# Projecting queries and keys of one batch at a time, in blocks of 256 columns

## The chip, the core and the metric

The kernel runs on one core of a Trainium2 chip, in one launch. The metric is the device time in microseconds (us) of that core, the median of repeated executions. Engines are named as in the profile: PE (TensorE, the matrix engine; PEld is its loading of stationary operands), DVE (VectorE), ACT (ScalarE), POOL (GpSimd) and SP (SyncE, which here only issues transfers). All data of this kernel are float32 unless said otherwise, and the engines wait for one another through semaphores.

## The reference, cut to what matters

The computation is a decoder of two layers on x of shape (8, 256, 512): eight batches of 256 tokens, 512 features. Each step is added to x and the sum is normalised over the features:

```python
x = _layernorm(x + _L0_attn_ref(x, ...))    # differential attention, causal
x = _layernorm(x + _L0_xattn_ref(x, ...))   # long convolution, with the context
x = _layernorm(x + _L0_ffn_ref(x, ...))     # experts, two for each token
x = _layernorm(x + _L1_attn_ref(x, ...))    # causal self attention, 16 heads of 32
x = _layernorm(x + _L1_xattn_ref(x, ...))   # cross attention
x = _layernorm(x + _L1_ffn_ref(x, ...))     # routed causal attention
```

The two stages that the change touches are both causal attentions. The first has 32 query heads of 16 features (taken in pairs, of which the second is subtracted with a learned factor) and 8 heads of keys; the self attention has 16 heads of 32:

```python
qkv = jnp.einsum('bsd,ed->bse', x, w_qkv)
q, k, v = ...                                   # 16 heads of 32 each
scores = jnp.einsum('bhqd,bhkd->bhqk', q, k) * HD ** (-0.5)
scores = jnp.where(causal, jnp.float32(-1000000000.0), scores)
a = jax.nn.softmax(scores, axis=-1)
ctx = jnp.einsum('bhqk,bhkd->bhqd', a, v)
return jnp.einsum('bsd,ed->bse', ctx.reshape(b, s, d), w_o)
```

## The kernel before, in words

**Tiles.** The 2048 tokens are 16 tiles x0 to x15 of 128 tokens by 512 features (P = 128, D = 512, KB = 4 blocks of 128 features, NT = 16). A batch is two tiles (S = 256 tokens), a group is two batches, so four tiles (TPG = 4, GT = 512 tokens), and there are four groups (NG = 4).

**Stages.** In the trace the first attention takes the span from 0 to about 490 us, the long convolution to 830, the experts to 1115, the self attention from 1115 to 1502, the cross attention to 1843, the routed attention the rest.

**Units and slots.** `causal_attention` (L1097) serves the three causal attentions. A unit is four heads of one batch: eight units to a batch in the first attention (`upb` 8), four in the self attention. The program runs through slots; in slot u it lays out for PE: the scores of unit u for the maxima (`maxima`, ps_q, L1151), the transposed weights of the unit `wait` slots before (`weights`, ps_k, L1214 and L1223), and the products with the values of the unit one slot before that (`products`, ps_pv, L1257 and L1267). Around a unit the other engines work: ACT copies the scores from PSUM to `rows` (L1160), POOL masks `rows` (affine_select, L1162), DVE takes the negated maximum `neg` (L1171); later ACT takes the exponential `pT` (L1231), POOL masks it (L1232), DVE takes the reciprocal sum (L1275). After the last unit of a batch `split` (L1178 to L1185) cuts the maxima into bfloat16 terms, and `turn` (ps_n, L1193) turns them on PE for the weights of that batch. The PSUM tile of the scores has one buffer, shared by ps_q and ps_k; `rows` has two buffers in the first attention and one in the self attention.

**Filling.** The projections of a group are a list of pieces, each with a slot by which it must have run and a list of steps (one matmul each, with an assumed cost). `prepare` makes the list. Pieces wait in `queue`, ordered by that due slot; `fill` puts steps into PE's order between scores, weights and products as long as a budget lasts; `need` runs what is due in the next slot. `at` registers other work for a place of a later slot ("start", "mid", "end"), or as output projections for "fill". So the order of the instructions on PE, DVE, ACT and POOL is written out by the program, and each of these engines executes in that order. SP's transfers are ordered by the scheduler.

**Projections.** Each group is turned: four transposes on PE to a tile, one PSUM tile `pt`, one ACT copy to `xT` (L195; `turned_group`, with one buffer for xT). `feature_block` (L1404) computes 128 output features for all 512 tokens of the group: four matmuls of 128x512, evicted by ACT (L1411) to qT or kT. In the first attention keys are one such block `ps_k`, evicted twice by ACT to `kz` with a mask `half` of one or the other half of each pair of heads (L323). Values are computed by tile.

**The start of the program.** `load_x` (L67) has SP load tiles 0 to 3; then Wk, Wq, Wv and Wo follow (L131, L248). Wq is reordered by eight copies on DVE (L269) and eight on POOL (L271) before queries can use it; `half` (L275) is reduced on DVE.

**The start of the self attention.** The experts leave their outputs in DRAM (`ys`). `combine` (L1064) makes three functions for a tile: `load` (SP loads x from DRAM, L1075, and POOL gathers two rows of ys for each token, L1077), `add` (two DVE additions L1086, then DVE statistics and two POOL instructions for the root, L139 and L140), and `norm` (DVE, L154). `self_attention` (L1437) does this for tiles 0 to 3 before the first slot. In `prepare` of group g the tiles of group g + 1 are registered one after the other: for the first group tiles 4 and 5 are gathered at the end of slot 0, tile 6 at the end of slot 1, tile 7 at the end of slot 2. The query and key blocks of column block c are due in slot c, the values of the first batch in slot 5, of the second in slot 7 (9 in the last group).

Of the kernel before, what the change touches and what calls it, by code (L numbers as in the profile page):

```python
# [5 lines left out]


# [2 lines left out]

# [6 lines left out]
F32 = mybir.dt.float32  # L17
# [6 lines left out]
P = 128  # L24
B, S, D = 8, 256, 512
NT = B * S // P
TPG = 4
NG = NT // TPG
GT = TPG * P
KB = D // P  # L30
# [3 lines left out]
H0, HD0 = 16, 16  # L34
LAMBDA_INIT = 0.8 - 0.6 * math.exp(-0.3 * 12)
H1, HD1 = 16, 32
# [13 lines left out]
def decoder_kernel(ctx: ExitStack, tc: tile.TileContext, a: dict, out: bass.AP):  # L50
    nc = tc.nc
# [15 lines left out]
    def load_x(tiles):  # L67
        for t in tiles:
            nc.sync.dma_start(out=x[t], in_=xin[:, t, :])

    load_x(range(TPG))

    ident = const.tile([P, P], F32, tag="ident", name="ident")
    make_identity(nc, ident)
# [97 lines left out]

    MM, TR = 0.86, 0.45

    def product_steps(tile, lhsT, rhs, done):

        ps = []

        def step(k):
            if k == 0:  # L180
                ps.append(tile())
            nc.tensor.matmul(  # L182
                ps[0], lhsT=lhsT(k), rhs=rhs(k), start=(k == 0), stop=(k == KB - 1)
            )
            if k == KB - 1:
                done(ps[0])

        return [(MM, lambda k=k: step(k)) for k in range(KB)]

    def turned(pools, dst, src, tag="mm"):  # L190

# [43 lines left out]
    def diff_attention():  # L235
# [6 lines left out]
        w = wpool.tile([P, 7168], F32, tag="w", name="w_l0")  # L242
        wk = load_w(w, 2048, a["L0_attn_Wk"], P)
        wq_in = load_w(w, 0, a["L0_attn_Wq"], D)
        wv = load_w(w, 2560, a["L0_attn_Wv"], P)
        wo = w[:, 3072:5120].rearrange("p (k c) -> p k c", k=KB)
        for t in range(4):
# [15 lines left out]
        wq = w[:, 5120:7168].rearrange("p (k c) -> p k c", k=KB)  # L263
# [35 lines left out]
        def prepare(work, pools, g, at, here):  # L299
            qT = work.tile([P, KB, GT], F32, tag="qT", name="qT")  # L300
            kz = work.tile([P, 2, GT], F32, tag="kz", name="kz")
            v = work.tile([P, TPG, P], F32, tag="v", name="v", bufs=3)
            xT, need = turned_group(work, pools, g)
# [12 lines left out]
            values_steps = [(MM, lambda ti=ti: values(ti)) for ti in range(TPG)]  # L316
            if g:

                need.append((0, values_steps))

            def keys(ps):
                for i in range(2):
                    nc.scalar.mul(kz[:, i, :], ps, half[:, i : i + 1])  # L323

            need.append(
                (
                    0,
                    product_steps(
                        lambda: pools.tile([P, GT], F32, tag="mm", name="ps_k"),
                        lambda k: wk[:, k, :],  # L330
                        lambda k: xT[0][:, k, :],
                        keys,
                    ),
                )
            )
            for c, first in enumerate((0, 1, 4, 5)):
                need.append((first, feature_block(pools, qT, xT, wq, 0, c, HD0**-0.5)))

            if g == 0:
                need.append((9, values_steps))  # L340
# [756 lines left out]
    def causal_attention(name, prepare, finish, upb=KB, gather=None):  # L1097
# [18 lines left out]
        with ExitStack() as st:  # L1116
# [175 lines left out]
            due = [0]  # L1292

            def at(slots, place, f):

                if place == "fill":
# [104 lines left out]
                fill(9.0)  # L1401
                happen("end")

    def feature_block(pools, r, xT, w, at, c, scale=1.0):  # L1404

        cs = slice(at + c * P, at + (c + 1) * P)
        return product_steps(
            lambda: pools.tile([P, GT], F32, tag="mm", name="ps_f"),
            lambda k: w[:, k, cs],
            lambda k: xT[0][:, k, :],  # L1410
            lambda ps: nc.scalar.mul(r[:, c, :], ps, scale),  # L1411
        )
# [23 lines left out]

    def self_attention(wqkv, wo, arrive):  # L1437

        for steps in zip(*[arrive(t) for t in range(TPG)]):
            for f in steps:  # L1440
                f()

        def prepare(work, pools, g, at, here):
            qT = work.tile([P, KB, GT], F32, tag="qT", name="qT")
            kT = work.tile([P, KB, GT], F32, tag="kT", name="kT")
            v = work.tile([P, TPG, D], F32, tag="v", name="v_s")
            xT, need = turned_group(work, pools, g)
            for c in range(KB):
                need.append((c, feature_block(pools, qT, xT, wqkv, 0, c, HD1**-0.5)))
                need.append((c, feature_block(pools, kT, xT, wqkv, D, c)))  # L1450

            if g + 1 < NG:
                for ti in range(TPG):
                    load, add, norm = arrive((g + 1) * TPG + ti)
                    first = max(0, 2 * KB * g - 1 + ti)
                    at(first - here, "end", load)
                    at(first - here + 1, "mid", lambda add=add: add(lambda f: at(0, "end", f)))
                    at(first - here + 2, "mid", norm)

            for ti in range(TPG):  # L1460
                need.append(
                    (
                        5 + ti // 2 * (4 if g == NG - 1 else 2),
                        token_block(
                            pools, xT, wqkv, 2 * D, ti,
                            lambda ps, ti=ti: nc.scalar.copy(v[:, ti, :], ps),
                        ),
                    )
                )
# [12 lines left out]

        causal_attention("s", prepare, finish)


# [257 lines left out]
    with ExitStack() as st_self:  # L1743
# [111 lines left out]
```

## Time and profile before

| What | us |
|---|---|
| Time before, median of 3 runs | 2199.62 (2196.56 to 2202.16) |
| The profiled execution, its own time | 2202.62 |
| Its span in the trace | 2200.8 |
| PE busy in it | 2053.4 (93%) |
| DVE, POOL, ACT busy | 1272.1, 824.4, 598.9 |
| Mean granted clock of PE | 0.97 |
| First attention, 0 to 490: PE busy | 433.1 |
| Self attention, 1115 to 1502: PE busy | 350.3 |

All rows but the first are from one execution; the span is what the trace covers, its own time has a little around it. In the lists of waits a line names the engine and the instruction that waited, after the arrow what released it, then the total, the number and the longest of these waits. In a timeline a row is a run of like instructions: its start, how long they took from first to last, engine and line, the written and the read tiles, the shape, the number, and in brackets how long the engine had been idle before and what ended that. The granted clock is given as a share of the full one. A matmul of this kernel's float32 operands appears as two records.

### The profile page before, as it was taken

How to read it: one execution, taken by the hardware profiler on the slowest of the kernel's cores; microseconds unless marked ns; L12 is line 12 of the kernel's file. 1: busy time of each engine (PE TensorE's matmuls, PEld its weight loads, DVE VectorE, ACT ScalarE, POOL GpSimd, SP SyncE). 2: the span in 40 equal slices, each digit the busy share in tenths (PEclk: the TensorE clock that was granted, in tenths of full speed). 3: DMA queues.
4: the chain of work that ended last, by engine and by line, in shares of the span. 5: the costliest groups of instructions: out<-in, count | busy, mean ns of one | idle time of the engine just before them, and what ended most of it. 6: DMA issues, size and time to landing. Idle time of an engine off the chain costs nothing. (4 is left out here: it accounts for less than half of the span.)

```text
span 2200.8 us, 35612 instructions
## 1 busy us (share of the span) xinstructions
PE 2053.4 (93%) x14904; PEld 1192.7 (54%) x14904; DVE 1272.1 (58%) x1923; ACT 598.9 (27%) x723; POOL 824.4 (37%) x918
## 2 busy tenths in 40 slices
PE   7989899879999999999959999999999999999995
PEld 4545555544453455555524444446877875445543
DVE  4676767758888964222235746466344343476777
ACT  4545545520010013111114333340110110333342
POOL 2566767737556723000033644343000000242343
PEclk9989999989999999999989999999999999999998
DMA  6899801335124144131140201002100100000000
GB/s 221 328 385 382 312 1 45 92 87 198 29 76 164 29 148 149 62 141 61 48 145 29 77 20 58 1 2 96 39 20 20 39 0 1 1 11 11 11 18 33
DMA packets 110032, 197.56 MB, mean 90 GB/s; under 512 B 7088, under 2 KB 30768, under 8 KB 109872
## 3 DMA queue, kind: packets, MB, share of 16 engines
q1 hardware_dynamic: 104752, 178.49, 23.4%
q0 software_dynamic: 5120, 16.78, 2.2%
q8 instruction: 120, 1.97, 0.4%
q14 instruction: 40, 0.33, 0.0%
HBM read 93.54 MB, written 112.20 MB: 93 GB/s over the span
## 5 line engine op out<-in xcount | busy, mean ns | idle before, releaser
L1275 DVE RECIPROCAL rsum<-ps_pv 128x256 f32<-128x256 f32 x128 | 224.4, 1753 | 238.1 <-PE ps_pv L1267 237.9
L171 PE MATMUL ps_y<-kv,wt 128*128 128x512 f32 x640 | 282.6, 600 | 4.4 <-POOL kv L519 3.8
L1231 ACT ACTIVATE pT<-ps_k 128x1536 f32<-128x1536 f32 x128 | 185.7, 1450 | 288.9 <-PE ps_k L1223 286.9
L1171 DVE TENSOR_REDUCE neg<-rows 128x12 f32<-128x1536 f32 x128 | 223.1, 1743 | 50.9 <-POOL rows L1162 50.9
L1160 ACT COPY rows<-ps_q 128x1536 f32<-128x1536 f32 x128 | 184.2, 1439 | 184.0 <-PE ps_q L1151 142.2
L1162 POOL TENSOR_SCALAR_AFFINE_SELECT rows<-rows 128x1024 f32<-128x1024 f32 x128 | 140.1, 1094 | 250.3 <-ACT rows L1160 250.0
L1232 POOL TENSOR_SCALAR_AFFINE_SELECT pT<-pT 128x1024 f32<-128x1024 f32 x128 | 141.1, 1102 | 242.9 <-ACT pT L1231 242.9
L171 PEld LDWEIGHTS ps_y<-kv,wt 128*128 128x128 f32 x640 | 120.9, 192 | 154.4 <-issue 135.8
L1242 POOL TENSOR_TENSOR pT<-pT 128x512 f32<-128x512 f32 x112 | 145.2, 1296 | 9.3
L1077 POOL DMA_INDIRECT w_l1x<-ys,slots x32 | 32.9, 1028 | 267.1 <-DMA ys<-y_m 259.2
L182 PE MATMUL ps_t<-w_l1f,xT 128*128 128x512 f32 x256 | 122.0, 611 | 0.0
L182 PE MATMUL ps_f<-xT,w_l1a 128*128 128x512 f32 x256 | 118.2, 604 | 2.9 <-ACT xT L195 2.9
L992 PE MATMUL po_m<-dn,hT 128*128 (+1 forms) x216 | 101.9, 609 | 1.5
L139 POOL TENSOR_SCALAR rstd<-bn_mv 128x1 f32<-128x1 f32 x80 | 16.9, 212 | 217.0 <-DVE bn_mv L145 211.2
L1267 PE MATMUL ps_pv<-pT,ones_v 128*32 128x256 f32 (+1 forms) x1152 | 85.0, 377 | 6.7 <-POOL pT L1242 6.3
L557 DVE TENSOR_REDUCE yc<-z 128x64 f32<-128x512 f32 x128 | 86.0, 673 | 6.2 <-POOL w_l1a L558 5.8
L1151 PE MATMUL ps_q<-kz,qT 32*128 32x128 f32 x1536 | 62.9, 294 | 22.6 <-ACT pT L1231 17.5
L1151 PEld LDWEIGHTS ps_q<-kT,qT 32*128 32x128 f32 x1536 | 49.9, 190 | 56.2 <-issue 17.0
L1151 PEld LDWEIGHTS ps_q<-kz,qT 32*128 32x128 f32 x1536 | 50.4, 192 | 54.8 <-ACT pT L1231 34.4
L182 PEld LDWEIGHTS ps_f<-xT,w_l1a 128*128 128x128 f32 x256 | 46.3, 189 | 54.8 <-issue 49.3
L1151 PE MATMUL ps_q<-kT,qT 32*128 32x128 f32 x1536 | 62.4, 292 | 12.5 <-ACT kT L1411 4.8
L974 DVE TENSOR_TENSOR h_b<-h_b,pg 128x352 f32<-128x352 f32 x36 | 18.8, 521 | 95.3 <-ACT h_b L973 95.3
(326 smaller groups left out, 3744.6 us busy)
## 6 DMA issues: line engine op xcount, KB each, us to landing
xs<-zero SPq DMA_DIRECT2D x8, 4352.0 KB, 31.3
ys<-zero SPq DMA_DIRECT2D x8, 4352.0 KB, 31.4
filters<-in_L_xattn_k SPq DMA_DIRECT2D x4, 2560.0 KB
first_h<-xs SPq DMA_DIRECT2D x36, 256.0 KB, 2.6
ys<-y_m SPq DMA_DIRECT2D x36, 256.0 KB, 2.0
gu<-in_L_ffn_gate_up_proj SPq DMA_DIRECT2D x3, 2816.0 KB, 19.8
wt<-filters SPq DMA_DIRECT2D x32, 256.0 KB, 2.8
x<-in_x SPq DMA_DIRECT2D x16, 256.0 KB, 4.9
```

What stands on the lines that cost most here:

```text
L171: nc.tensor.matmul(ps, lhsT=lhsT(k), rhs=rhs(k), start=(k == 0), stop=(k == n - 1))
L182: nc.tensor.matmul(ps[0], lhsT=lhsT(k), rhs=rhs(k), start=(k == 0), stop=(k == KB - 1))
L557: nc.vector.tensor_reduce(yc[:, lb], z, AX.X, ALU.add)
L992: nc.tensor.matmul(po, lhsT=hT[:m, i, :], rhs=dn[i][:m, bass.ds(e, 1), :], start=(i == 0), stop=(i == len(FCH) - 1),)
L1151: nc.tensor.matmul(block[:, s, j, :], lhsT=q(rows, c, b * S + i * P, P), rhs=k(rows, c, b * S + keys * P, P), start=True, stop=True,)
L1160: nc.scalar.copy(d.rearrange("p j s k -> p s j k"), block)
L1162: nc.gpsimd.affine_select(out=rows, in_=rows, compare_op=ALU.is_ge, fill=-FAR, base=0, pattern=[[0, 8], [-1, P]], channel_multiplier=1,)
L1171: return lambda: nc.vector.tensor_reduce(neg[u // upb % 2][:, :, :, c], d, AX.X, ALU.max, negate=True)
L1231: nc.scalar.activation(p[:, 0:3].rearrange("p j s q -> p s j q"), block, AF.Exp)
L1232: nc.gpsimd.affine_select(out=p[:, 0:2].rearrange("p j s q -> p (j s) q"), in_=p[:, 0:2].rearrange("p j s q -> p (j s) q"), compare_op=ALU ...
L1242: nc.gpsimd.tensor_tensor(p[:, 3], p[:, 1], p[:, 2], ALU.add)
L1275: nc.vector.reciprocal(r, ps[:, 1, :])
```

## The change

The diff does three things.

1. At the start, SP loads tiles 0 and 1, then Wk and Wq, then tiles 2 and 3, then Wv and the rest.
2. In the first attention, the queries of all four groups are computed by batch: blocks of 128 features by 256 tokens, with those of the second batch due eight slots after those of the first. In group 0 the keys too are two blocks of 256 tokens; those of the second batch are due in slot 8, the transposes of tiles 2 and 3 in slot 7. In the other groups the keys stay one block of 512 tokens.
3. In the self attention, queries and keys of all groups are computed by batch in blocks of 256 tokens, the second batch's due four slots after the first's. Before the first slot only tiles 0 and 1 are gathered, added and normalised. Tiles 2 and 3 come in slots 0 to 2 (loaded in slot 0, added in slot 1, normalised in slot 2), and the second batch's pieces of group 0 are put into the queue at the start of slot 3, through a new place "due" of `at`. The first batch's transposes stay at the head of a group, those of the second are due in the slot of its first blocks.

`product_steps` is given the cost of a step, which is half for a block of half the tokens.

The diff, cut to its core:

```diff
-    load_x(range(TPG))
+    load_x(range(2))
...
         wq_in = load_w(w, 0, a["L0_attn_Wq"], D)
+        load_x(range(2, TPG))
         wv = load_w(w, 2560, a["L0_attn_Wv"], P)
...
+            def keys(tokens):
+                def done(ps):
+                    for i in range(2):
+                        nc.scalar.mul(kz[:, i, tokens], ps, half[:, i : i + 1])
...
             if g:
-                need.append((0, values_steps))
...
+                need = turns + [(0, values_steps), (0, keys(slice(0, GT)))]
+            else:
+                need = turns[:2] + [(0, keys(batches[0]))]
+                need += [(7, steps) for _, steps in turns[2:]]
+                need += [(8, keys(batches[1])), (9, values_steps)]
+            for b, tokens in enumerate(batches):
+                for c, first in enumerate((0, 1, 4, 5)):
+                    block = feature_block(pools, qT, xT, wq, 0, c, HD0**-0.5, tokens)
+                    need.append((8 * b + first, block))
+            need.sort(key=lambda piece: piece[0])
...
+                if place == "due":
+                    at(slots, "start", lambda: insort(queue, f, key=lambda piece: piece[0]))
...
-    def feature_block(pools, r, xT, w, at, c, scale=1.0):
+    def feature_block(pools, r, xT, w, at, c, scale=1.0, tokens=slice(0, GT)):
         cs = slice(at + c * P, at + (c + 1) * P)
+        n = tokens.stop - tokens.start
         return product_steps(
-            lambda: pools.tile([P, GT], F32, tag="mm", name="ps_f"),
+            lambda: pools.tile([P, n], F32, tag="mm", name="ps_f"),
             lambda k: w[:, k, cs],
-            lambda k: xT[0][:, k, :],
-            lambda ps: nc.scalar.mul(r[:, c, :], ps, scale),
+            lambda k: xT[0][:, k, tokens],
+            lambda ps: nc.scalar.mul(r[:, c, tokens], ps, scale),
+            MM * n / GT,
         )
...
-        for steps in zip(*[arrive(t) for t in range(TPG)]):
-            for f in steps:
-                f()
+        with tc.manual_schedule(engines={mybir.EngineType.DVE, mybir.EngineType.Pool}):
+            first = [arrive(t) for t in range(2)]
+            for load, _, _ in first:
+                load()
+            roots = []
+            for _, add, _ in first:
+                add(roots.append)
+            for root, (_, _, norm) in zip(roots, first):
+                root()
+                norm()
...
+            def arriving(t, slot, place):
+                load, add, norm = arrive(t)
+                at(slot - here, place, load)
+                at(slot - here + 1, "mid", lambda: add(lambda f: at(0, "end", f)))
+                at(slot - here + 2, "mid", norm)
...
+            for b in range(2):
+                tokens = slice(b * S, (b + 1) * S)
+                pieces = [(b * KB, steps) for _, steps in turns[2 * b : 2 * b + 2]]
+                for c in range(KB):
+                    slot = b * KB + c
+                    pieces.append(
+                        (slot, feature_block(pools, qT, xT, wqkv, 0, c, HD1**-0.5, tokens))
+                    )
+                    pieces.append((slot, feature_block(pools, kT, xT, wqkv, D, c, 1.0, tokens)))
+                late = 9 if g == NG - 1 else 7
+                for ti in range(2 * b, 2 * b + 2):
+                    pieces.append(value(ti, late if b else 5))
+                pieces.sort(key=lambda piece: piece[0])
+                if g == 0 and b == 1:
+                    for t in range(2, TPG):
+                        arriving(t, 0, "mid")
+                    for piece in pieces:
+                        at(3, "due", piece)
+                else:
+                    need += pieces
```

More of the change, by code (lines that the diff above doesn't have):

```diff
@@ L8 @@
 import math
+from bisect import insort
 from contextlib import ExitStack
@@ L173, in decoder_kernel, with product_steps @@
     MM, TR = 0.86, 0.45
-    def product_steps(tile, lhsT, rhs, done):
+    def product_steps(tile, lhsT, rhs, done, cost=MM):
         ps = []
@@ L186, in step @@
                 done(ps[0])
-        return [(MM, lambda k=k: step(k)) for k in range(KB)]
+        return [(cost, lambda k=k: step(k)) for k in range(KB)]
     def turned(pools, dst, src, tag="mm"):
@@ L302, in prepare @@
             v = work.tile([P, TPG, P], F32, tag="v", name="v", bufs=3)
-            xT, need = turned_group(work, pools, g)
+            xT, turns = turned_group(work, pools, g)
+            batches = [slice(b * S, (b + 1) * S) for b in range(2)]
             def values(ti, ps=[]):
@@ L316, in prepare @@
             values_steps = [(MM, lambda ti=ti: values(ti)) for ti in range(TPG)]
-            if g:
-                need.append((0, values_steps))
[L321 to L330, printed above, removed]
-                        lambda k: xT[0][:, k, :],
[L332 to L340, printed above, removed]
+            def keys(tokens):
[3 more added lines that the diff above has]
+                n = tokens.stop - tokens.start
+                return product_steps(
+                    lambda: pools.tile([P, n], F32, tag="mm", name="ps_k"),
+                    lambda k: wk[:, k, :],
+                    lambda k: xT[0][:, k, tokens],
+                    done,
+                    MM * n / GT,
+                )
+            if g:
+                need = turns + [(0, values_steps), (0, keys(slice(0, GT)))]
[8 more added lines that the diff above has]
+            need.sort(key=lambda piece: piece[0])
             if g == NG - 1:
@@ L1294, in at @@
             def at(slots, place, f):
-                if place == "fill":
+                if place == "due":
+                    at(slots, "start", lambda: insort(queue, f, key=lambda piece: piece[0]))
+                elif place == "fill":
                     after.append((now[0] + slots, f))
@@ L1402, in causal_attention @@
                 happen("end")
-    def feature_block(pools, r, xT, w, at, c, scale=1.0):
+    def feature_block(pools, r, xT, w, at, c, scale=1.0, tokens=slice(0, GT)):
         cs = slice(at + c * P, at + (c + 1) * P)
+        n = tokens.stop - tokens.start
         return product_steps(
-            lambda: pools.tile([P, GT], F32, tag="mm", name="ps_f"),
+            lambda: pools.tile([P, n], F32, tag="mm", name="ps_f"),
             lambda k: w[:, k, cs],
-            lambda k: xT[0][:, k, :],
-            lambda ps: nc.scalar.mul(r[:, c, :], ps, scale),
+            lambda k: xT[0][:, k, tokens],
+            lambda ps: nc.scalar.mul(r[:, c, tokens], ps, scale),
+            MM * n / GT,
         )
@@ L1446, in prepare @@
             v = work.tile([P, TPG, D], F32, tag="v", name="v_s")
[L1447 to L1450, printed above, removed]
+            xT, turns = turned_group(work, pools, g)
+            def arriving(t, slot, place):
[3 more added lines that the diff above has]
+                at(slot - here + 2, "mid", norm)
@@ new lines, in value @@
+            def value(ti, slot):
+                return slot, token_block(
+                    pools, xT, wqkv, 2 * D, ti, lambda ps: nc.scalar.copy(v[:, ti, :], ps)
+                )
+            need = []
+            for b in range(2):
[5 more added lines that the diff above has]
+                        (slot, feature_block(pools, qT, xT, wqkv, 0, c, HD1**-0.5, tokens))
+                    )
+                    pieces.append((slot, feature_block(pools, kT, xT, wqkv, D, c, 1.0, tokens)))
[10 more added lines that the diff above has]
+                    need += pieces
@@ L1452, in prepare @@
+            need.sort(key=lambda piece: piece[0])
             if g + 1 < NG:
                 for ti in range(TPG):
[L1454 to L1469, printed above, removed]
+                    arriving((g + 1) * TPG + ti, max(0, 2 * KB * g - 1 + ti), "end")
```

## The prediction

> **What bounds the kernel now.** I read the page first (busy times), then the waits of TensorE, then the timeline at the two places the change touches, then windows of those places for the granted clock.
>
> ```profile
> PE 2053.4 (93%) x14904; PEld 1192.7 (54%) x14904; DVE 1272.1 (58%) x1923; ACT 598.9 (27%) x723; POOL 824.4 (37%) x918
> ```
>
> TensorE is busy 93% of 2200.8 us, so only its idle time (147 us) and its slow clock can be won. The waits of PE (total us, times, longest) say where a part of that idle time is:
>
> ```profile
> PE ps_q L1151 <- ACT pT L1231: 22.1, 18, 1.6
> PE pt L194 <- DVE x L154: 20.6, 1, 20.6
> PE ps_n L1193 <- DVE terms L1182: 12.4, 7, 4.6
> ```
>
> The first row is slots with no projection left to fill them: scores wait for the exponential of the slot before (16.5 us of it in the first attention, 4.6 in the self attention). The second is the start of the self attention, the third the split of the maxima; its first instance closes the first eight units. The start (columns: start, duration, engine, line, instruction, [idle before <- releaser]):
>
> ```profile
> 9.12 6.56 PE L182 MATMUL ps_k<-xT,w_l 128*128 128x512 f32 x8 [0.67 <-ACT xT L195]
> ...
> 11.97 1.87 DVE L269 COPY w_l<-w_l 128x128 f32<-128x128 f32 x8 [9.34 <-DMA w_l<-in_L_attn_Wq]
> ...
> 15.52 3.60 PE L182 MATMUL ps_f<-xT,w_l 128*128 128x512 f32 x8
> ...
> 19.80 0.95 PE L1151 MATMUL ps_q<-kz,qT 32*128 32x128 f32 x24 [0.69 <-ACT qT L1411]
> ...
> 51.63 0.40 PE L1193 MATMUL ps_n<-ident_b,terms 128*32 128x128 bf16 x8 [1.62 <-DVE terms L1182]
> ```
>
> Four tiles are turned, keys of 512 columns run at half clock (0.82 us a matmul against 0.45 in the next row), and Wq lands at about 11.95. The same view at the self attention:
>
> ```profile
> 1135.01 3.48 PE L194 MATMUL pt<-ident,x 128*128 128x128 f32 x16 [20.61 <-DVE x L154]
> ...
> 1146.98 0.95 PE L1151 MATMUL ps_q<-kT,qT 32*128 32x128 f32 x24 [0.69 <-ACT kT L1411]
> ...
> 1150.78 1.02 POOL L1077 DMA_INDIRECT w_l1x<-ys,slots  x1 [0.18 <-issue]
> ...
> 1160.70 1.72 DVE L1171 TENSOR_REDUCE neg<-rows 128x12 f32<-128x1536 f32 x1
> ...
> 1177.59 0.95 PE L1151 MATMUL ps_q<-kT,qT 32*128 32x128 f32 x24
> ```
>
> **The change, part 1: the start of the first attention.** Half a megabyte less is ahead of Wq; the window 3 to 12 us moves 253 to 337 GB/s, so Wq lands 1.6 to 2.0 us earlier, at about 9.9. On SP's queue the loads of tiles 2 and 3 (about 0.45 us each to issue) now stand ahead of Wv; the first values that read Wv run at 35 us, and tiles 2 and 3 are turned after 21 us, so neither is late. Two tiles are turned instead of four; keys are 4 steps of 256 columns. The 256-column price is from another row, 64 such matmul records in 13.81 us (ps_x L171): 0.216 each warm, 0.43 cold, two records to a step, so 3.4 us, from 6.35 to 9.75. POOL's half of the Wq copies that the first query block needs takes 1 us, so queries start at about 10.95 and take 1.7 us (warm) to 3.4 (cold). The keys' eviction needs `half`, which now stands behind DVE's eight copies (1.87) of Wq: it can't end before 13.0. First scores between 13.3 and 15.0; I take 14.4, against 19.80: 5.4 earlier. Of that, some goes back: tiles 2 and 3 are turned ahead of slot 3 and their copies wait on ACT behind the row copy of 1.44 us (about 2 us of idle PE). Going slot by slot with scores 0.88, a 256-column block 1.73, row copy 1.44, affine 1.09, maximum 1.75, the eighth unit's split releases ps_n at 47.8 instead of 51.63. **Gain 3.8** (2.5 to 5.4).
>
> **Part 2: the rest of the first attention.** Queries of all groups come in 256-column blocks with the second batch's due 8 slots later. Laying the built order of TensorE's instructions of both kernels side by side, and giving each slot without filling 1.6 us and each short one 1.6 minus its filling, I count 17.3 us of waits before (the trace: 16.5) and 13.4 after: **+4.0** (2 to 5). An empty slot also cools the clock: the window 270 to 280 has a granted clock of 0.72. Fewer of these dips: **+1.6** (0 to 3). Price: 128 records of 512 columns at 0.428 become 256 at 0.216, **−0.5**. ACT's 16 query evictions of 0.60 become 32 of about 0.40: 3 us more on an engine busy 27%, hidden by its idle time; uncovered, at most that 3 us. Sum of the first attention: **+8.9** (4 to 12).
>
> **Part 3: the start of the self attention.** Only tiles 0 and 1 are gathered and normalised: DVE's adds of them (0.75 each) follow the second gather of tile 0, which landed at 1126.1; norms at 1130.1 and 1131.3; transposes from 1130.7 (before: 1135.01); the first scores at about 1138.1 (before: 1146.98). That is 8.9 us. SP's sixteen loads of x keep their order and cost nothing new. But what was taken out comes back in slot 0. POOL gets, right behind the affine of slot 0, eight gathers (tiles 2 and 3, and 4 and 5 as before) in place of four, at the 1.28 us pitch of the rows from 1150.78 on. Issued from 1142 to 1152, the last lands 3.4 to 3.9 us after its issue (as those of before did), at about 1154.7. Behind them on POOL waits the affine of unit 1. On DVE, eight adds and four statistics stand ahead of `neg` of unit 1, which can therefore not start before 1156.4 and ends at 1158.15. The score rows have a single buffer here, so ACT's row copy of unit 2 waits for that `neg` (to 1159.65), behind it on ACT the evictions of the fourth column block (0.8), and behind those scores of unit 3, at 1160.55. PE has had nothing since 1152.0: the value blocks are behind this slot's scores in its order. **A stall of 8.5 us.** Then unit 3's row copy waits for `neg` of unit 2 (1164.25), and on ACT, behind it, the xT copies of tiles 2 and 3, on which the second batch's blocks wait: 2.9 us more. The scores of unit 4 come at about 1172.2 instead of 1177.59, 5.4 early, but 24 steps of the second batch's blocks (48 records of 0.216, 10.4 us), done by then before, are still owed: **−5.0** (−8 to 0).
>
> Here the clock matters.
>
> ```profile
> 1135.00:1137.00 2.00, 1.99 (x9) 1.73 (x10) 1.44 (x4) 0.58 (x1) 1.36 (x3) 0.50 0.11 42
> 1137.00:1138.00 1.00, 1.00 (x7) 0.73 (x6) 0.55 (x1) 0.61 (x2) 0.10 (x1) 0.55 0.00 0
> 1138.00:1140.00 2.00, 1.33 (x6) 0.73 (x6) 0.00 (x0) 1.11 (x2) 0.00 (x0) 1.00 0.00 0
> ```
>
> The third column from the end is the granted clock: full 2.9 us after the first transpose. [...]
>
> **Part 4: the rest of the self attention.** Idle by the same count of slots: 12.3 before, about 11 after (empty slots become rarer, but eight blocks behind fresh transposes wait 0.8 to 1.9 for the xT copies, six times): +1.3. Cold stretches (the window from 1250 to 1260 has 0.83; eight value matmuls took 4.94 against 3.70) go from about 5 us to 3.8: +1.2. Columns: 256 records at 0.428 become 512 at 0.216: −0.9. ACT evictions go from 32 of 0.60 to 64 of 0.40, 6.4 us more on an idle engine. **+1.6** (−6 to +4, the lower end if waits and clock go against it).
>
> **Sum.** 8.9 − 5.0 − 1.0 + 1.6 = 4.5 us less. The profiled execution took 2202.62 (span 2200.8), so 2198.1 for one like it; the median shown is 3.0 below that: **2195**.
>
> **Rivals.** *Start holds, self attention breaks even* (0.19): the gathers land earlier than I have it and the owed work fills slots that would be empty (four of them before, 1.5 each). Then −5.0 and −1.0 become about +1, sum 11 to 12: 2188. For it: empty slots exist after; against it: the DVE order is fixed, and `neg` stands behind the adds. *Slower by the clock* (0.28): in the self attention the PE, after the stall and after each wait for fresh xT copies, runs at half rate. Place: 1160 to 1178, 13 us of work, up to +6.5 us; then four transposing slots at up to 2.5 each. With 9 to 11 us of it on top of the stall, where I have net 0.2, the sum is about −5 to −8: 2207. It decides from 4.5 us of cold time more than I count on. For it: 0.50 until 1137, dips with 1.6 us waits; against it: 1140 to 1180 ran at 1.00 with 0.7 us waits. *The start doesn't move* (0.10): Wq lands no earlier since x tiles 2 and 3 share the queues; then part 1 gives 1 and the sum is 1.7: 2198.
>
> **How the numbers follow.** My case has 0.43, with its own range 2191 to 2200. A measurement of this kernel can tell about 0.3% (6.6 us) from no change: faster is below 2193.0, slower above 2206.2. Faster (0.34): rival one's 0.17 and two fifths of my case's 0.43 (0.17). Slower (0.28): rival two's 0.25 and 0.03 of the rest. Within: 0.38. The range for 8 in 10 goes from 2185 (parts 1 to 4 near their good ends) to 2210 (rival two with the xT waits doubled).
>
> **What would show it.** First scores near 14.4 and ps_n near 47.8; waits of ps_q on pT about 4 us shorter in the first attention. In the self attention first scores near 1138, eight gathers from 1142, `neg` of unit 1 after 1156, an idle PE of some 8 us before unit 3's scores, scores of unit 4 near 1172. I am wrong if that idle stretch is missing or twice as long, or if the granted clock between 1160 and 1500 falls below 0.95 on the mean.

## The result

The changed kernel is slower: 2206.77 us (2205.67 to 2210.83) against 2201.08 us (2196.56 to 2206.25) of the kernel before, ratio 1.0031 with a 95% interval of 1.0018 to 1.0043, so 4 to 9 us. The prediction was 2195, faster. Its profiled execution took 2210.02 us, 7.4 more than that of before.

The profile after: the busy line of its page, and the waits of PE that answer to those shown of before (engine, tile, line, releaser: total us, times, longest).

```profile
PE 2059.9 (93%) x15296; PEld 1269.0 (57%) x15296; DVE 1277.1 (58%) x1923; ACT 605.1 (27%) x773; POOL 827.6 (37%) x918
```

```profile
PE pt L195 <- DVE x L155: 16.5, 1, 16.5
PE ps_q L1158 <- ACT pT L1238: 13.3, 12, 1.6
PE ps_n L1200 <- DVE terms L1189: 12.8, 6, 4.6
PE ps_q L1158 <- ACT kT L1422: 11.4, 7, 8.7
PE ps_f L183 <- ACT xT L196: 11.2, 8, 3.7
```

Two waits shrank as intended: the start of the self attention (20.6 to 16.5) and the empty slots (22.1 to 13.3). Two grew: scores behind ACT's kT (4.8 to 11.4, one of them 8.7) and blocks behind fresh copies of xT (2.9 to 11.2), by 14.9 together against the 12.9 that was won. Smaller waits shrank as well, so over the whole span PE's idle time is nearly the same (147.4 and 148.4 us). Of the 7.5 us by which the span is longer, 6.5 are busy time: PE took longer for its work.

By stages (us in one profiled execution each). Here the first attention goes up to the first product of the long convolution (ps_y), the self attention from its first gather to the first product with the values in the cross attention (po_x), and the routed attention from the last such product to the end; the stages of the introduction are cut elsewhere:

| Stage | before | changed | difference | predicted |
|---|---|---|---|---|
| First attention | 497.1 | 491.7 | -5.4 | -8.9 |
| Convolution and experts | 620.9 | 620.7 | -0.2 | 0 |
| Self attention | 446.4 | 456.0 | +9.6 | +4.4 |
| Cross attention | 261.1 | 261.1 | 0 | 0 |
| Routed attention | 375.3 | 378.8 | +3.5 | 0 |

In the self attention 5.6 of the 9.6 us are idle time of PE (38.1 and 43.7) and 4.0 busy time (408.3 and 412.3); in the routed attention, whose code is unchanged, all 3.5 are busy time.

The start of the first attention, in the timeline of the changed kernel (start, duration, engine, line, instruction, [idle before <- releaser]):

```profile
15.29 1.19 PE L1158 MATMUL ps_q<-kz,qT 32*128 32x128 f32 x24 [0.47 <-ACT qT L1422]
...
25.21 0.20 ACT L295 ACTIVATE lam<-lam 128x2 f32<-128x2 f32 x1 [3.47 <-DVE lam L294]
25.32 1.42 ACT L1167 COPY rows<-ps_q 128x1536 f32<-128x1536 f32 x1
...
28.05 1.13 PE L183 MATMUL ps_k<-xT,w_l 128*128 128x256 f32 x4 [3.04 <-ACT xT L196]
29.11 1.35 PE L1158 MATMUL ps_q<-kz,qT 32*128 32x128 f32 x24
...
52.52 0.30 PE L1200 MATMUL ps_n<-ident_b,terms 128*32 128x128 bf16 x8 [2.94 <-DVE terms L1189]
```

First scores came 4.5 us earlier, the release of the first split 0.9 later. On ACT the row copy of unit 2 stood behind an exponential (L295). It belongs to the lambda chain, a few small instructions that compute the learned factor of the first attention, and it waited 3.47 us for DVE, where the scaling of Wo and the maximum of unit 1 stood ahead of its products. The copies of the second batch's tiles stood behind that row copy; PE waited 3.04 us for them and then ran slow (24 score matmuls in 1.35 instead of 0.95).

The start of the self attention:

```profile
1134.27 0.95 PE L1158 MATMUL ps_q<-kT,qT 32*128 32x128 f32 x24 [0.47 <-ACT kT L1422]
...
1138.07 1.02 POOL L1084 DMA_INDIRECT w_l1x<-ys,slots  x1 [0.18 <-issue]
...
1153.90 1.72 DVE L1178 TENSOR_REDUCE neg<-rows 128x12 f32<-128x1536 f32 x1
...
1155.71 1.44 ACT L1167 COPY rows<-ps_q 128x1536 f32<-128x1536 f32 x1 [11.35 <-DVE neg L1178]
...
1157.76 1.66 PE L1158 MATMUL ps_q<-kT,qT 32*128 32x128 f32 x24 [8.75 <-ACT kT L1422]
1159.36 1.97 PE L195 MATMUL pt<-ident,x 128*128 128x128 f32 x8
...
1165.03 5.94 PE L183 MATMUL ps_f<-xT,w_l1a 128*128 128x256 f32 x16 [3.70 <-ACT xT L196]
...
1174.33 0.95 PE L1158 MATMUL ps_q<-kT,qT 32*128 32x128 f32 x24
```

The chain is the predicted one: gathers from 1138, the maximum of unit 1 behind the adds at 1153.90, the row copy of unit 2 behind it, an idle PE of 8.75 us. What was too small in the sum is the clock. Windows of the changed kernel (after the window its length and the busy time of PE; the third column from the end is the granted clock):

```profile
1130.00:1132.00 2.00, 2.00 (x6) 1.56 (x5) 0.00 (x0) 0.00 (x0) 0.00 (x0) 0.50 0.00 0
...
1152.49:1169.56 17.07, 8.09 (x43) 6.58 (x44) 15.78 (x26) 4.80 (x7) 10.41 (x17) 0.50 0.20 59
```

It was at half ("cold") for the first blocks, and again for 17.07 us from 1152.49 on: the blocks of the second batch took 5.94 us for 16 records instead of 3.45 (the predicted 0.216 each).

### The profile page after: what moved, and what is told of

Same layout as the page of the kernel before. It is cut to its first block, busy times and chain, and to the rows that moved or that the text cites. A ratio compares the mean times of both kernels' runs of the same rounds, so it can differ in the third digit from the quotient of the medians.

```text
span 2208.3 us, 36443 instructions
## 1 busy us (share of the span) xinstructions
PE 2059.9 (93%) x15296; PEld 1269.0 (57%) x15296; DVE 1277.1 (58%) x1923; ACT 605.1 (27%) x773; POOL 827.6 (37%) x918
## 5 line engine op out<-in xcount | busy, mean ns | idle before, releaser
L183 PE MATMUL ps_f<-xT,w_l1a 128*128 128x256 f32 x512 | 128.2, 398 | 11.2 <-ACT xT L196 11.2
L183 PEld LDWEIGHTS ps_f<-xT,w_l1a 128*128 128x128 f32 x512 | 96.3, 195 | 32.7 <-ACT xT L196 13.4
L1158 PE MATMUL ps_q<-kz,qT 32*128 32x128 f32 x1536 | 62.9, 294 | 14.3 <-ACT pT L1238 13.3
L1158 PE MATMUL ps_q<-kT,qT 32*128 32x128 f32 x1536 | 62.2, 292 | 14.4 <-ACT kT L1422 11.4
```

What stands on the lines that cost most here:

```text
L183: nc.tensor.matmul(ps[0], lhsT=lhsT(k), rhs=rhs(k), start=(k == 0), stop=(k == KB - 1))
L1158: nc.tensor.matmul(block[:, s, j, :], lhsT=q(rows, c, b * S + i * P, P), rhs=k(rows, c, b * S + keys * P, P), start=True, stop=True,)
```

## The experiments

Those that were timed ran in four sets on three chips, on which the kernel before took 2216.0, 2203.2, 2201.6 and 2214.6 us; a difference below is the ratio within its set, in us, with its 95% interval.

### The two parts alone

One kernel has only the first attention's part, one only the self attention's. Against the changed kernel:

```diff
  first attention's part alone: self_attention as before
-        with tc.manual_schedule(engines={mybir.EngineType.DVE, mybir.EngineType.Pool}):
-            first = [arrive(t) for t in range(2)]
...
+        for steps in zip(*[arrive(t) for t in range(TPG)]):
  self attention's part alone: diff_attention as before
-    load_x(range(2))
+    load_x(range(TPG))
-        load_x(range(2, TPG))
...
```

> Only the first attention's part of the change (the loads' order too); the self attention as before. Theory A (gains and losses stay in their stages): the first attention ends 5.6 us earlier, as the two profiles show, and nothing else moves: about -5.6 us, ratio 0.9975. Inside it, scores of unit 9 at 54 us as before (the start gives nothing), the gain comes at units 16 to 46. [...]

> Only the self attention's part of the change. Theory A: self attention 9.6 us longer from its first gather to the first product of the cross attention, total about +9.6, ratio 1.0044. Theory B: the 3.3 us that the routed attention lost in the profile of the changed kernel belong to this part too: +13, ratio 1.006. The idle time of PE before the scores of unit 3 is about 8.7 us in both.

First part: -4.7 us (-6.6 to -2.7). Self part: +11.1 (+6.9 to +15.3), with 455.9 us in the self attention and the wait of 8.2 before unit 3. So the loss is the self attention's, and the parts add up to +6.4. The changed kernel beside a later set gave the same:

> The changed kernel as it is, beside the repaired one on the same chip. By the sum of its parts (-4.8 and +11) +6 us, ratio 1.003; against the repaired kernel 12 to 15 us slower. If the parts don't add, within 3 us of before.

It measured +7.3 (+4.0 to +10.4). The first theory of the first run holds for its time, not in its detail: in that run's profile the split's release came at 48.06. One profile does not tell much here, since with the start as before the release came anywhere from 47.35 to 51.81, as the first scores did from 15.80 to 19.99; the way from the first scores to the release is steadier (31.6 to 32.3 there).

### The first attention: where its gain is

```diff
-            if g:
-                need = turns + [(0, values_steps), (0, keys(slice(0, GT)))]
+            if g:      # by batch, as changed
...
+            else:      # group 0: four tiles, keys and queries of 512, as before
+                need = turns + [(0, keys(slice(0, GT))), (9, values_steps)]
+                for c, first in enumerate((0, 1, 4, 5)):
+                    need.append((first, feature_block(pools, qT, xT, wq, 0, c, HD0**-0.5)))
```

> First attention: queries by batch only in groups 1 to 3; group 0, the loads and the self attention as before. Theory A (the gain comes from slots that were empty and are now filled, the start gives nothing): first attention 4 to 6 us shorter, ratio 0.9975. Theory B (it is group 0 with its queries of batch 1 moved back that fills the empty slots 16 to 19): 1 to 3 us shorter, ratio 0.999.

-3.8 us (-6.2 to -1.6), first attention 490.2. Most of the part's gain (-4.7) comes without any change to the start: filled slots, as the prediction's second part said. The two intervals overlap, so that the start itself gave anything is not shown; by the medians it is 0.9 us. Two more kernels ask what holds the start. In one, the lambda vectors are loaded right behind Wq:

```diff
         wq_in = load_w(w, 0, a["L0_attn_Wq"], D)
+        lv = const.tile([P, 4, HD0], F32, tag="lv", name="lv")
+        (four loads of lv)
         load_x(range(2, TPG))
```

> The first attention's part alone, with the four lambda vectors loaded right behind Wq, ahead of tiles 2 and 3. Theory A (the lambda chain on DVE and its exponential on ACT stood in front of the row copy of unit 2 and made the transposed tiles late): scores of unit 3 at 27 instead of 29.1 us, release of the first split 1.5 to 2 us earlier than 52.5; total 1 to 3 us better than the part alone: -6 to -8, ratio 0.997. Theory B (the next limit, the row copies and maxima of units 4 to 7, takes it all): -5, ratio 0.998, first split at 52 to 53 us.

+0.7 us (-3.1 to +4.4): the edit failed for a reason of its own. The exponential now stood ahead of the second tile's copy on ACT, which waited for it, and first scores came at 21.07. In the other, the chain is moved instead:

```diff
-        nc.vector.tensor_scalar(wo, wo, lnw, 1.0 - LAMBDA_INIT, ALU.mult, ALU.mult)
-        (lambda chain)
+        def late_factors():    # both of them
...
+            if g == 0:
+                at(8, "end", late_factors)
```

> The first attention's part alone, with the scaling of Wo and the whole lambda chain (eight small instructions on DVE, one exponential on ACT) moved from before the first slot to the end of slot 8. Theory A (that chain, waiting for its vectors, stood ahead of the row copy of unit 2 on ACT): from the scores of unit 0 to those of unit 3 11.5 us or less instead of 13.6 to 13.8, to the release of the first split 33.5 instead of 35.4 to 37.2; total 1 to 2 us better than the part alone: -6, ratio 0.997. Theory B (PE's own work in slots 3 to 7 is the limit): distance to the split as before, total -4 to -5.

```profile
14.82 0.95 PE L1162 MATMUL ps_q<-kz,qT 32*128 32x128 f32 x24 [1.75 <-ACT qT L1426]
...
26.66 0.95 PE L1162 MATMUL ps_q<-kz,qT 32*128 32x128 f32 x24
...
48.44 0.41 PE L1204 MATMUL ps_n<-ident_b,terms 128*32 128x128 bf16 x8 [2.94 <-DVE terms L1193]
```

That timeline shows 11.84 us from unit 0 to unit 3 and 33.62 to the release, against 13.57 and 35.35 of the part alone: the chain did cost 1.7 us. (With the vectors loaded early the way to the release was 33.62 too.) In time it is -5.3 us (-7.7 to -2.6), not to be told from the part alone.

### The self attention: start or later groups

The blocks by batch stay, but all four tiles are gathered before the first slot:

```diff
+        for steps in zip(*[arrive(t) for t in range(TPG)]):
+            for f in steps:
+                f()
...
-                if g == 0 and b == 1:
-                    for t in range(2, TPG):
-                        arriving(t, 0, "mid")
-                    for piece in pieces:
-                        at(3, "due", piece)
-                else:
-                    need += pieces
+                need += pieces
```

> Self attention alone: blocks of 256 columns by batch in all groups, but all four tiles gathered, added and normalised before the first slot, as in the kernel before. Theory A (the loss is made by bringing the second batch in behind the first slots): start as before, rest of the stage within 2 us of before: 0 to +2 us, ratio 1.000 to 1.001. Theory B (the blocks by batch lose by themselves: they wait for fresh copies of xT, and twice as many instructions): +5 us or more, ratio 1.0025.

+0.7 us (-3.3 to +4.6), self attention 444.1. Then the start as changed, with blocks of 512 columns in groups 1 to 3:

```diff
+            else:      # g > 0
+                need = turns
+                for c in range(KB):
+                    need.append((c, feature_block(pools, qT, xT, wqkv, 0, c, HD1**-0.5)))
+                    need.append((c, feature_block(pools, kT, xT, wqkv, D, c)))
```

> Self attention alone: two tiles first and blocks by batch in group 0 only; groups 1 to 3 in blocks of 512 columns as before. Theory A (the loss is group 0's): as the full self part, +9 to +12 us, ratio 1.0045, with the stall of 8 us before the scores of unit 3. Theory B (the loss is in the later groups): +3 to +5 us, ratio 1.002.

+18.9 us (+12.3 to +25.3), self attention 461.2. The loss is made in group 0. That the blocks by batch of the later groups win some of it back is likely but not shown: the profiles differ by 5.3 us (461.2 and 455.9; PE's idle time 50.6 and 44.4), but the intervals of the two times overlap.

### The stall: gathers, adds or the one buffer

Tiles 4 to 7 are gathered later:

```diff
-                    arriving((g + 1) * TPG + ti, max(0, 2 * KB * g - 1 + ti), "end")
+                    arriving((g + 1) * TPG + ti, 2 * KB * g - 1 + ti if g else 2 + ti, "end")
```

> The self attention's part alone, with the gathers of tiles 4 to 7 in slots 2 to 5 instead of 0, 0, 1, 2. Theory A (eight gathers and eight adds ahead of the maximum of unit 1 make the stall): that maximum starts about 1 us after the adds of tiles 2 and 3, idle PE before the scores of unit 3 falls from 8.7 to 2 to 3 us, total about +3, ratio 1.0015. Theory B (the two tiles of batch 1 alone are enough for the stall, or it moves to unit 4): idle before units 3 and 4 together stays above 8 us, total +8 or more, ratio 1.004.

+12.4 us (+9.1 to +15.7): no better, though the wait before unit 3 fell from 8.2 to 2.1 as the first theory said. A second measurement:

> The self part alone with the gathers of tiles 4 to 7 in slots 2 to 5, a second time: its profile had a self attention 4.3 us shorter than the part as it is, its time did not. Theory A (the profile is right, six executions were too few): +3 to +7 us, ratio 1.002. Theory B (the gathers later harm in a place that the profile did not show): +10 or more, ratio 1.005.

+12.8 us (+7.1 to +18.4). This is the second theory's +10 or more. The timeline shows where a part of it went: the same chain, with the tiles that now arrive in slots 4 to 7.

```profile
1214.44 1.72 DVE L1172 TENSOR_REDUCE neg<-rows 128x12 f32<-128x1536 f32 x1
...
1216.25 1.44 ACT L1161 COPY rows<-ps_q 128x1536 f32<-128x1536 f32 x1 [2.43 <-DVE neg L1172]
1217.59 1.08 ACT L196 COPY xT<-pt 128x512 f32<-128x512 f32 x2
...
1218.72 2.93 PE L183 MATMUL ps_f<-xT,w_l1a 128*128 128x256 f32 x6 [3.62 <-ACT xT L196]
```

A maximum behind an add, a row copy behind the maximum, the xT copies behind the row copy, PE idle for 3.62 us and slow after it (these 6 records took 2.93 us; at 0.216 each it would be 1.3). Next, a second buffer for the rows, gathers as changed:

```diff
-  d = work.tile([P, 3, 4, P], F32, tag="rows", name="rows", bufs=1 if name == "s" else 2)
+  d = work.tile([P, 3, 4, P], F32, tag="rows", name="rows", bufs=2)
-  r = work.tile([P, D], F32, tag="row", name="res", bufs=3)
+  r = work.tile([P, D], F32, tag="row", name="res", bufs=bufs)      # 2 in the self attention
```

> The full self part with two buffers for the score rows (paid for by two instead of three buffers of the residual row in this stage). Theory A (the single buffer ties unit 3's scores to the maximum of unit 1): the row copy of unit 2 no longer waits for that maximum, scores of unit 3 about 8 us after those of unit 2 fall to 5 us, idle time 8.2 goes to 2 or less there; the wait comes back one unit later (row copy of unit 3 waits for the maximum of unit 1, about 2 us). Self attention 4 to 6 us shorter than with the part as it is: total +4 to +7, ratio 1.0025. Theory B (POOL's affine behind the gathers stops the chain whatever the buffers): no more than 2 us better, +9, ratio 1.004.

```profile
1151.63 0.95 PE L1152 MATMUL ps_q<-kT,qT 32*128 32x128 f32 x24 [0.47 <-ACT kT L1416]
1158.22 1.97 PE L195 MATMUL pt<-ident,x 128*128 128x128 f32 x8 [5.64 <-DVE x L155]
1160.86 5.79 PE L183 MATMUL ps_f<-xT,w_l1a 128*128 128x256 f32 x16 [0.68 <-ACT xT L196]
```

+4.8 us (+1.1 to +8.8), self attention 449.1. The wait before unit 3 is gone (0.47), so the one buffer was the link between the adds and PE. A wait comes back right behind these scores, as 5.64 us before the transposes of tile 2, whose norm stands behind the same adds on DVE; the clock is cold after it (0.74 on the mean from 1154.40 to 1174.40; transposes in 1.97, blocks in 5.79). Both repairs together:

> The self part alone, with both repairs: tiles 4 to 7 gathered in slots 2 to 5, and two buffers for the score rows (two instead of three of the residual row). Theory A (both waits of the start are gone, so the earlier first scores count): scores of unit 4 at 50 us or less after the first gather (59.6 before, 61.9 changed), self attention 442 to 447 us against 444 to 449 before: -3 to +2 us, ratio 0.9995. Theory B (the second batch's copies of xT stand behind row copies on ACT, and cold clock after each wait): +4 to +8, ratio 1.003.

```profile
1149.70 0.95 PE L1152 MATMUL ps_q<-kT,qT 32*128 32x128 f32 x24 [0.47 <-ACT kT L1416]
1150.66 1.11 PE L195 MATMUL pt<-ident,x 128*128 128x128 f32 x8
1153.18 3.72 PE L183 MATMUL ps_f<-xT,w_l1a 128*128 128x256 f32 x16 [1.41 <-ACT xT L196]
...
1160.27 0.95 PE L1152 MATMUL ps_q<-kT,qT 32*128 32x128 f32 x24
```

-2.4 us (-5.3 to +0.2), self attention 443.8, with 35.0 us of idle PE in it against 38.1 before. Behind the first scores no wait above 1.5 us is left at the start, the second batch's transposes and blocks run at full clock (1.11 and 3.72 us; 1.00 from 1151.20 to 1171.20), and the scores of unit 4 come 49.0 us after the first gather. Neither repair does it alone; with both, the self part stops losing. That it wins is not shown, as the interval reaches zero.

### Whole versions

First, the change with the four tiles gathered first in the self attention:

> The whole change except for the start of the self attention: there all four tiles are gathered first, as before. Theory A (first attention's gain of 4 to 6 us holds, self attention's start was the whole loss, its later groups by batch give 0 to 3): -4 to -8 us, ratio 0.997. Theory B (clock and later stages swallow the gains): -2 to +1, ratio 1.000.

-2.2 us (-5.3 to +0.9), nearest to the second theory; the interval reaches to the first. Then the change with all three repairs:

> The whole change with the three repairs: lambda chain and scaling of Wo at the end of slot 8 of the first attention; in the self attention tiles 4 to 7 gathered in slots 2 to 5 and two buffers for the score rows. Theory A (the parts add): -5.3 from the first attention and -2.4 from the self attention, -6 to -9 us, ratio 0.9965. Theory B (cold clock and later stages swallow a part): -3 to -5, ratio 0.998.

-6.9 us (-9.7 to -4.0), ratio 0.9969 (0.9956 to 0.9982). It is faster than both kernels: in the same set the changed one was at 1.0033. The parts add.

### An untouched stage

The time of the later gathers alone was some 8 us worse than its self attention, so four more executions were profiled for their stages.

> The kernel before, once more, for its stages. Theory A (the length of the routed attention after the last product of the cross attention, 375.3 us in the first profile, belongs to the kernel): 375 to 376 again. [...]

> As the look before: 375 to 376 if it belongs to the kernel, 375 to 383 if it is drawn in every execution. The self attention 444 to 449 us from first gather to first product of the cross attention.

> The self part with later gathers (tiles 4 to 7 in slots 2 to 5), once more for its stages: self attention 451 to 452 us as in its two profiles. Routed attention: 380 to 383 if that belongs to this kernel (then it makes up the 8 us that its time is worse than its self attention), 375 to 383 if it is drawn.

> The self part with later gathers and two buffers of score rows, once more for its stages: self attention 443 to 446 us. Routed attention 376 to 377 as in its first profile if it belongs to the kernel, 375 to 383 if it is drawn.

Routed attention: 375.3 and 375.3 in the kernel before, as the first time; with later gathers 380.0 (383.1 and 380.0 in its earlier profiles); with both repairs 383.0 (376.7 in its earlier profile). So it is neither fixed by the kernel nor drawn freely. Its code is the same in all twenty profiles, its length went from 375.2 to 383.3; the last section shows what went with it. Self attention: 448.9 twice (kernel before), 451.1 (later gathers), 442.4 (both repairs), the last just below what was expected. In the three profiles with later gathers the routed attention was 4.7 to 7.8 us longer than the 375.3 of the kernel before; that most of the 8 us lies there in executions without a profile is not shown and stays open.

## Why the prediction was wrong

Two terms failed: in part 1 the "about 2 us of idle PE", in the sum the "− 1.0", which stands for the clock after the stall of part 3.

**Part 1 (+3.8 predicted) gave -0.9 in the profile.** First scores at 15.29 instead of 14.4: 0.9. From there to the release 37.23 us instead of 33.4. Two terms were missing: the lambda chain ahead of the row copy of unit 2 (1.7, shown by moving it), and the clock after the 3.04 us wait. The first part alone has the same wait at the same place with the clock at full (1.00 in the 4 us after it), and needs 35.35, which is 1.9 less. With the chain moved the way is 33.62, almost the predicted one. So the step that failed is "about 2 us of idle PE": the copies' queue on ACT was followed, but not what stands ahead of those copies, an exponential waiting for DVE.

**Part 2 (+5.1) was right.** In the profile the first attention stood 0.2 us behind at unit 9 and ended 5.4 ahead; the variant that leaves group 0 alone shows it in time (-3.8). The waits of scores for the exponential went from 17.5 to 13.3 in this stage (the prediction reads 16.5 where the trace has 17.5).

**Part 3 (-5.0, and -1.0 for the clock) had the right chain and the wrong price.** The self attention began 5.6 us earlier in the changed kernel, so times are counted from its first gather. The idle stretch was 8.75 against 8.5 predicted. Scores of unit 4 were to be 5.4 early and were 2.4 late. Of these 7.8 us, 1.8 came with the first scores (7.1 us earlier instead of 8.9; their cold blocks took 5.58 us for 16 records instead of 3.45); from unit 3 to unit 4 it took 16.57 us instead of 11.65, of which 0.7 are scores at half clock, 0.8 a longer wait for xT, 2.5 the cold blocks; the rest, some 2 us, is not split.

The clock after the stall is the mis-sized term. No run shows the 1.0, which was the author's estimate; in its place the changed kernel showed 3.8. In the 17.07 us at half clock PE did little, but its rows took 3.8 us more than like rows at full clock (scores 1.66 instead of 0.95, transposes 1.97 instead of 1.11, blocks 5.94 instead of 3.72). It belongs to the stall: the four profiles with an idle stretch of 8.1 to 9.0 us at this place (the changed kernel twice, its self part, and that part with later groups as before) all have 17.1 us at half clock behind it, the seven with the self attention of before have none there (in the kernel before 1.00 from 1140 to 1180), and neither have the two of the self part with both repairs. (The whole version with all repairs has one of 6.8 us, behind a wait of 2.75 us for the copies of xT.)

The sum has no term for cold first blocks, and luck had a part in that. In the eleven profiles that start with two tiles the first scores came 8.5 to 10.1 us after the first transpose, where the prediction has 7.4 (1130.7 to 1138.1). But the full clock that was read 2.9 us after the first transpose belongs to one execution: in the seven profiles with the self attention of before the clock opened 2.9 to 4.2 us after the first transpose in three and 8.7 to 9.3 us after it in four, among these two more of the very kernel before. So that kernel pays for cold first blocks as well in most of its profiles (first scores after 14.4 to 14.7 us instead of 12.0 to 12.4). In one of them transposes start at 1137.45, and the clock stays at half:

```profile
1137.50:1146.00 8.50, 7.83 (x21) 4.78 (x22) 1.93 (x5) 2.34 (x4) 1.41 (x3) 0.50 0.07 27
```

In the three where it opened early, nothing but transposes ran between the idle stretch and the opening. One row of one execution was read as a rule; what the opening depended on was not shown.

In sum: with 4.7 us less from part 1, 3 more for the clock after the stall and 1.8 for the first blocks, 4.5 us of gain become a loss of about 5.

**Part 4 (+1.6) was not contradicted:** with four tiles first, blocks by batch gave 444.1 and 444.9 us of self attention, against 443.6 to 449.3 for the same stage as before.

**The rivals and the signs.** "Slower by the clock" (2207) named the place, the mechanism and nearly the time. "The start doesn't move" happened too, for another reason than given: Wq came earlier (its copies began at 10.61 instead of 11.97), and what was won was lost behind other instructions. The signs named for being wrong did not show: the idle stretch had its length, and the mean granted clock from 1160 to 1500 was 0.99, not below 0.95. A mean over 340 us does not see ten at half clock.

## What to carry to other kernels

Starting a pipeline with half its data moves the other half's loads, adds and copies into the in-order queues of the first steps: for each engine list what now stands ahead of the first reduction and the first copy, small setup work included, and check which single buffer ties that engine to the matrix engine. Repair such a chain at all its links and look again, because a wait taken from one place showed up at the next. And price an idle matrix engine by its idle time plus the slow stretch that may follow, which here (3.8 us) was nearly as large as the sum that was to be won; read the clock from several executions before one row is taken as a rule.

## What the hardware showed beside

The same idle gap did not always cool the clock. PE waited 3.04 us at the same point of the same code in two kernels: in the changed one the wait ended at 28.05 and the clock was 0.69 on the mean from 28 to 32, in the first part alone it ended at 25.21 and the clock was 1.00 from 25 to 29. Windows of the changed kernel, the second at half clock, then of the first part alone:

```profile
26.10:29.51 3.41, 1.46 (x16) 1.08 (x20) 1.57 (x1) 1.90 (x4) 1.09 (x1) 1.00 1.05 389
29.51:32.92 3.41, 3.41 (x26) 2.74 (x23) 0.18 (x1) 1.86 (x3) 0.86 (x1) 0.50 0.63 244
```

```profile
21.00:25.00 4.00, 1.18 (x10) 0.86 (x8) 1.63 (x5) 2.62 (x5) 1.02 (x1) 1.00 0.99 340
25.00:29.00 4.00, 3.79 (x37) 3.08 (x38) 1.75 (x1) 1.81 (x3) 0.22 (x2) 1.00 0.92 339
```

So the length of a wait did not tell what the clock did after it, and what decided it was not shown.

An untouched stage ran at different clocks too. In the routed attention the first 32 small matmuls, shortly after a wait of 1.65 and 1.64 us, took 3.75 us at a granted clock of 0.98 in the kernel before and 6.56 us at 0.54 in the changed one:

```profile
1844.26 3.75 PE L171 MATMUL ps_g<-w_l1f,xT 128*128 128x16 f32 x32
```

```profile
1848.30 6.56 PE L172 MATMUL ps_g<-w_l1f,xT 128*128 128x16 f32 x32
```

Over the twenty traces, in order of the time that these 32 took:

| First 32 matmuls, us | Profiles | Routed attention, us |
|---|---|---|
| 3.74 to 3.89 | 6 | 375.2 to 375.4 |
| 5.68 and 5.70 | 2 | 376.7 |
| 5.71 to 5.87 | 3 | 380.0 to 380.1 |
| 5.91 to 6.19 | 7 | 383.0 to 383.3 |
| 6.56 | 1 | 378.8 |
| 6.70 | 1 | 375.4 |

The six profiles in which they ran fast have the short stage; of the fourteen in which they ran slow all but one have a longer one. It does not go by the kernel: the self part with both repairs has 376.7 in one profile and 383.0 in the other. So a stage that an edit does not touch differed by up to 8 us between profiles; a sum over stages can't forecast that, and it is about as large as the change that was to be measured.
